# Softmax division moved from each head pair's value sum to the output product of 128 queries

## The chip, the cores and the metric

The kernel runs on one core of one Trainium2 chip. The metric is the device time of one execution in microseconds; lower is better.

## The reference

Three parts work on `x` of shape (4, 1024, 256), each adding to the running result: a linear recurrence, an attention part, and a gated sparse feed-forward part that is used twice, ahead of the attention and behind it (called f1 and f2 in the kernel). The change lies in the attention:

```python
q = (x @ Wq.T).reshape(b, t, N_HEADS, HEAD_DIM)          # 8 heads of 64
kv_latent = x @ Wkv_down.T                                # 64 wide
k = (kv_latent @ Wk_up.T).reshape(b, t, N_HEADS, HEAD_DIM)
v = (kv_latent @ Wv_up.T).reshape(b, t, N_HEADS, HEAD_DIM)
scores = jnp.einsum('bqhd,bkhd->bhqk', q, k) * scale
attn = jax.nn.softmax(scores, axis=-1)
out = jnp.einsum('bhqk,bkhd->bqhd', attn, v)
return out.reshape(b, t, N_HEADS * HEAD_DIM) @ Wo.T
```

A softmax row is exp(s - max) divided by the sum of those exponentials. The sum over keys with the values is linear, so the division may be done at any point between the exponentials and the product with `Wo`. It has to be done per query and head.

## The kernel before, in words

The key and value up-projections are folded into the query and output weights, so that keys and values are the 64-wide latent itself. Four things run one after the other: the recurrence; the start of f1 with the first attention weights; a long stage (about 378 to 1331 us) in which the attention of four batches is the main thread and the rest of f1 and the first steps of f2 are side threads; and f2 (1331 us to the end).

In the long stage `heads()` is a generator that yields once per score tile. It loops over halves `nb` of a batch's 1024 queries, head pairs `g`, and query tiles `q` of 128 queries; inside, over the two heads `j` of the pair. One step is: four matmuls (L881) give scores of 128 queries by 1024 keys in a PSUM tile `sc`; DVE takes the negated row maximum `nm` (L885); ACT takes the exponential into `pr` and accumulates the row sum (L889). The exponentials must then be turned so that keys lie on partitions. For odd `q` the PE does it (`ptp`, L900) and ACT or DVE copies the result to `p` (L903, L905). For even `q` ACT rounds to fp16 (L892), POOL computes the remainder (L893), and a transposing DMA issued by SP brings both to `d` (L894).

The value sums are done later, in `values_sum()`, from two lists: `pending` for odd `q` (one step later) and `late` for even `q` (some steps later). A sum is 32 fp32 matmuls or 48 fp16 matmuls, 64 columns of the array for each head (L925), into a PSUM tile `pmo`. `heads()` is made anew for each batch, and what is left in both lists is summed at the end of each batch (L912).

The division of before: DVE takes the reciprocal of the two row sums (L919), POOL spreads each over 64 columns into `rows` (L921), the PE transposes `rows` into the second half of `pmo` (L933), ACT copies that to `rb` (L935), and DVE multiplies the sum by `rb` into `on` (L936), an SBUF tile that holds four head pairs of 128 queries.

`output()` takes `on` when all four pairs are there: ACT casts it to `onp0` (L945), POOL computes the rest `onp1` (L946), 12 matmuls form the product with the output weights (`pmy`, by `products`, L170), DVE adds it to `x` (L948).

PSUM has three rings in this stage: `sc` with two score tiles, `t` with two tiles for `ptp`, and `s` with two tiles for everything else: `pmo`, `pmy`, the query products and all side threads. Tiles of a ring are given out in the order in which the program asks.

`merge()` sets that order: after each step of `heads()` it takes the side generators that are due. A side entry is (first step, generator, distance to its next step). On top of this a scheduler orders each engine's instructions by simulated time, so that instructions of neighbouring steps can pass each other. `output()` of the first half of a batch is due at step 33 of 64, with a distance of 1.5; that of the second half 1.5 steps into the next batch, for the last batch one step before its end. The last batch's last two query tiles come after `merge()`, followed by the last half of `f2.head`.

Of the kernel before, what the change touches and what calls it, by code (L numbers as in the profile page):

```python
# [10 lines left out]
F32 = mybir.dt.float32  # L11
I32 = mybir.dt.int32
F32R = mybir.dt.float32r
BF16 = mybir.dt.bfloat16
F16 = mybir.dt.float16
AF = mybir.ActivationFunctionType
ALU = mybir.AluOpType
# [4 lines left out]
P = 128  # L22
B = 4
# [6 lines left out]
HEADS = 8  # L30
HD = 64
PAIRS = HEADS // 2
# [132 lines left out]
def products(nc, dst, pairs, start=True, stop=True):  # L165


    terms = [(x, y) for a, b in pairs for x, y in ((a[0], b[0]), (a[0], b[1]), (a[1], b[0]))]
    for i, (x, y) in enumerate(terms):
        nc.tensor.matmul(dst, x, y, start=start and i == 0, stop=stop and i == len(terms) - 1)  # L170
# [19 lines left out]
STEPS = 64  # L190
# [582 lines left out]
class Attention:  # L773
    def __init__(self, tc, x, ident, ident64, wqk, wvo, wd, sp, wp):
        self.nc, self.x, self.ident, self.ident64 = tc.nc, x, ident, ident64
        self.wqk, self.wvo, self.wd, self.sp, self.wp = wqk, wvo, wd, sp, wp
        self.hp = None
        self.k, self.xnt, self.qs, self.on = {}, {}, {}, {}

        self.sident = wp.tile([HD, HD], F32R, tag="sident", name="sident")  # L780

# [71 lines left out]
            nc.vector.tensor_tensor(qs[other, j, :], pm[mine, :], qs[mine, j, :].bitcast(F32), ALU.subtract)  # L853
        yield

    def heads(self, b, psum):

        nc, sp, wp = self.nc, self.sp, self.hp  # L860
        kh, kl, la, lb = self.k[b]
        late, pending = [], []
        for nb, g, q in ((nb, g, q) for nb in range(2) for g in range(PAIRS) for q in range(4)):
            by_dma = q % 2 == 0
            if g == 0:
                self.on[b, nb, q] = wp.tile([P, PAIRS, P], F32, tag=f"on{q}", name=f"on{q}")
            qs = self.qs[b, nb, g]
            ssum = sp.tile([P, 2], F32, tag="ssum", name="ssum", bufs=4)
            if by_dma:
                pts = [wp.tile([P, 2 * TPB, P], F16, tag=f"d{j}", name=f"d{j}", bufs=2) for j in range(2)]  # L870
                parts = ((0, lb[0]), (TPB, lb[0]), (0, lb[1]))
                terms = [(v[:, c, :], i + c) for c in range(TPB) for i, v in parts]
            else:
                pts = [wp.tile([P, TPB, P], F32, tag=f"p{j}", name=f"p{j}") for j in range(2)]
                terms = [(la[:, c, :], c) for c in range(TPB)]
            for j in range(2):
                sc = psum.tile([P, T], "sc", "sc")
                for i, kk in enumerate((kh, kl)):
                    for kb in range(2):
                        sl = slice(kb * 512, (kb + 1) * 512)  # L880
                        nc.tensor.matmul(  # L881
                            sc[:, sl], qs[:, j, q * P : (q + 1) * P], kk[:, sl], start=(i == 0), stop=(i == 1)
                        )
                nm = sp.tile([P, 1], F32, tag="nm", name="nm", bufs=4)
                nc.vector.tensor_reduce(nm, sc, AX.X, ALU.max, negate=True)  # L885
                if by_dma:
                    nc.vector.tensor_scalar(nm, nm, PSHIFT * math.log(2.0), None, ALU.add)  # L887
                pr = wp.tile([P, T], F32, tag="pr", name="pr", bufs=3)
                nc.scalar.activation(pr, sc, AF.Exp, bias=nm, accum_out=ssum[:, j : j + 1])  # L889
                if by_dma:  # L890
                    pd = wp.tile([P, 2, T], F16, tag="pd", name="pd", bufs=2)
                    nc.scalar.copy(pd[:, 0, :], pr)  # L892
                    nc.gpsimd.tensor_tensor(pd[:, 1, :], pr, pd[:, 0, :], ALU.subtract)  # L893
                    nc.sync.dma_start_transpose(pts[j], pd.rearrange("p i k -> p (i k)"))  # L894
                else:
                    for half in range(2):
                        pt = psum.tile([P, 4, P], "t", "ptp")
                        for kk in range(4):
                            kc = 4 * half + kk
                            nc.tensor.transpose(pt[:, kk, :], pr[:, kc * P : (kc + 1) * P], self.ident)  # L900
                        dst = pts[j][:, 4 * half : 4 * half + 4, :]
                        if half == 0 and b == B - 1:
                            nc.vector.tensor_copy(dst, pt)  # L903
                        else:
                            nc.scalar.copy(dst, pt)  # L905
                if j == 0 and pending:
                    self.values_sum(*pending.pop(0), psum)
                if j == 1 and late and by_dma:
                    self.values_sum(*late.pop(0), psum)
                yield  # L910
            (late if by_dma else pending).append((pts, terms, ssum, self.on[b, nb, q][:, g, :]))
        for args in late + pending:  # L912
            self.values_sum(*args, psum)

    def values_sum(self, pts, terms, ssum, on, psum):

        nc, sp = self.nc, self.sp
        rs = sp.tile([P, 2], F32, tag="rs", name="rs")
        nc.vector.reciprocal(rs, ssum)  # L919
        rows = sp.tile([P, 2, HD], F32, tag="rows", name="rows")  # L920
        nc.gpsimd.tensor_copy(rows, rs[:, :, None].to_broadcast([P, 2, HD]))  # L921
        po = psum.tile([P, 2, P], "s", "pmo")
        for n, (v, c) in enumerate(terms):
            for j in range(2):
                nc.tensor.matmul(  # L925
                    po[j * HD : (j + 1) * HD, 0, :],
                    v,
                    pts[j][:, c, :],
                    start=(n == 0),
                    stop=(n == len(terms) - 1),  # L930
                )

        nc.tensor.transpose(po[:, 1, :], rows.rearrange("p j d -> p (j d)"), self.ident)  # L933
        rb = sp.tile([P, P], F32, tag="rb", name="rb", bufs=1)
        nc.scalar.copy(rb, po[:, 1, :])  # L935
        nc.vector.tensor_tensor(on, po[:, 0, :], rb, ALU.mult)  # L936

    def output(self, b, nb, psum, tiles=range(4)):

        nc = self.nc  # L940
        for q in tiles:
            xt = self.x[b * TPB + nb * 4 + q]
            py = psum.tile([P, D], "s", "pmy")
            on = [self.hp.tile([P, PAIRS, P], F32R, tag=f"onp{i}", name=f"onp{i}") for i in range(2)]
            nc.scalar.copy(on[0], self.on[b, nb, q])  # L945
            nc.gpsimd.tensor_tensor(on[1], self.on[b, nb, q], on[0].bitcast(F32), ALU.subtract)  # L946
            products(nc, py, [([t[:, g, :] for t in on], [t[:, g, :] for t in self.wvo]) for g in range(PAIRS)])
            nc.vector.tensor_tensor(xt, xt, py, ALU.add)  # L948
            yield

# [78 lines left out]
def tile_kernel(ctx: ExitStack, tc: tile.TileContext, x_in, w_lru, vecs_in, rows, w_ffn, lin_t, w_attn, w_down, out):  # L1029
    nc = tc.nc  # L1030
# [31 lines left out]
    f2 = Ffn("f2", tc, bp, x, w)  # L1062

    with ExitStack() as c1:
        psum = Banks(c1.enter_context(tc.tile_pool(name="ps1", space=PSUM)), {"pu": 2, "po": 2, "py": 2, "pt": 2})
# [15 lines left out]
        for k in range(NBLK):  # L1081
# [11 lines left out]
            b = k // CH + 1  # L1093
# [24 lines left out]
    with ExitStack() as c2:  # L1118
# [51 lines left out]
        fp = c2.enter_context(tc.tile_pool(name="f_s", bufs=2))  # L1170
        side = []
        for b in range(B):
            n = STEPS * b
            side += [
                (n + nb * 32 + 8 * g - 7, at.queries(b, nb, g, psum, "s"), 1)
                for nb in range(2)
                for g in range(PAIRS)
                if b or nb or g
            ]
            side.append((n + 33, at.output(b, 0, psum), 1.5))  # L1180
            side.append((n + STEPS - 1 if b == B - 1 else n + STEPS + 1.5, at.output(b, 1, psum, range(2 if b == B - 1 else 4)), 1 if b == B - 1 else 1.5))
            side.append((n + 40 if b == B - 1 else n + STEPS + 24, f2.head(2 * b, sp, psum, "s"), 2))
            last = b == B - 1
            side.append((n + STEPS if last else n + STEPS + 8, f2.head(2 * b + 1, sp, psum, "s", (0,) if last else (0, 1)), 1 if last else 2))
            if b < B - 1:
                side.append((n + 38, chain(at.prepare(b + 1, 0, psum, "s"), at.values(b + 1, 0, psum, "s")), 1.5))
                side.append((n + 56, chain(at.prepare(b + 1, 1, psum, "s"), at.values(b + 1, 1, psum, "s")), 1.5))
        side.append((1, at.values(0, 1, psum, "s"), 1))
        for i in range(TPB, NT):
            n = i - TPB  # L1190
            start = 1 + 6.75 * n if n < TPB else STEPS * (n // TPB) - STEPS + 48.25 + 8 * (n % TPB + 1)
            side.append((start, f1.tile(i, fp, psum, "sss", parts=wfs, fine=True), [1, 1, 1, 1, 1, 2, 1]))
        merge(chain(*(at.heads(b, psum) for b in range(B))), side)
        run(at.output(B - 1, 1, psum, range(2, 4)), f2.head(NBLK - 1, sp, psum, "s", (1,)))
    with ExitStack() as c3:
        psum = Banks(c3.enter_context(tc.tile_pool(name="ps3", space=PSUM)), {"pl": 2, "px": 3, "pf": 3})
# [105 lines left out]
```

## Time and profile before

| | |
|---|---|
| median of 3 runs | 1536.99 us (1534.27 to 1539.68) |
| the profiled execution | 1533.81 us, span 1532.1 us |
| mean granted PE clock | 0.941 |
| busy, share of the span | PE 85%, DVE 77%, ACT 66%, POOL 44% |
| instructions | PE 10136, DVE 3674, ACT 2145, POOL 848 |

The shares are averages over all four parts of the kernel. A row of a group names the line, the engine, the operation, the tile written and the tiles read, then the number of instructions, their busy time together and the mean time of one, and last the idle time of the engine just before them with what ended it. A wait is given as "engine, tile, line waited for engine, tile, line: us in total, times, longest". PE means matmuls and transposes, DVE VectorE, ACT ScalarE, POOL GpSimd, SP the queue that issues the DMAs here.

### The profile page before, as it was taken

The page shows a single profiled execution, that of the slowest core. Times are in us where ns is not written, and L with a number is a line of the kernel's source. Part 1 is how long each engine was busy: PE and PEld are TensorE (multiplying, and loading weights), DVE is VectorE, ACT ScalarE, POOL GpSimd, SP SyncE. Part 2 cuts the span into 40 slices and gives each one's busy share as a digit, 9 for nine tenths or more (in the row PEclk, how much of TensorE's full clock was granted, in tenths as well). Part 3 has the DMA queues.
Part 4 walks back from the last instruction along what each step waited for, and adds up shares of the span by engine and source line. Part 5 has one row for each costly group of instructions (what it writes and reads, how often), then busy time and mean ns, then how long its engine had stood idle before and what let it go on. Part 6 is the DMA issues. An engine that isn't in the chain of part 4 may idle for free. (4 is left out here: it accounts for less than half of the span.)

```text
span 1532.1 us, 28693 instructions
## 1 busy us (share of the span) xinstructions
PE 1297.4 (85%) x10136; PEld 960.2 (63%) x10136; DVE 1182.9 (77%) x3674; ACT 1014.5 (66%) x2145; POOL 681.6 (44%) x848
## 2 busy tenths in 40 slices
PE   4879998698898898898998889888999998657786
PEld 3635455365676766766776767677777776334554
DVE  8976665697878887878778687777676675499998
ACT  5353433664787777787777787877777776476664
POOL 2033333162545454544543554454443534157776
PEclk9999999698999999999999999999999999789888
DMA  3010000331454334344433345434444454000000
GB/s 117 32 41 15 21 21 14 135 101 44 76 91 90 70 70 80 67 80 77 85 76 60 65 85 81 66 60 85 78 75 88 83 95 83 1 11 24 25 25 28
DMA packets 288609, 96.51 MB, mean 63 GB/s; under 512 B 268233, under 2 KB 284626, under 8 KB 288466
## 3 DMA queue, kind: packets, MB, share of 16 engines
q1 hardware_dynamic: 283024, 88.50, 29.0%
q10 hardware_dynamic: 5442, 6.18, 1.2%
q8 instruction: 80, 1.31, 0.3%
q14 instruction: 63, 0.52, 0.1%
HBM read 16.01 MB, written 11.53 MB: 18 GB/s over the span
## 5 line engine op out<-in xcount | busy, mean ns | idle before, releaser
L893 POOL TENSOR_TENSOR pd<-pr,pd 128x1024 f16<-128x1024 f32 x128 | 273.5, 2142 | 256.5 <-ACT pd L892 198.6
L885 DVE TENSOR_REDUCE nm<-sc 128x1 f32<-128x1024 f32 x256 | 308.5, 1218 | 76.8 <-PE sc L881 75.3
L889 ACT ACTIVATE pr<-sc,nm 128x1024 f32<-128x1024 f32 x256 | 285.9, 1120 | 89.8 <-DVE nm L887 53.3
L881 PE MATMUL sc<-kh,qs 128*128 128x512 f32 x512 | 184.9, 439 | 27.1 <-ACT pr L889 19.5
L881 PE MATMUL sc<-kl,qs 128*128 128x512 f32 x512 | 162.4, 398 | 0.0
L674 DVE MATCH_REPLACE8 wk<-m,wk 128x256 f32<-128x256 f32 x384 | 158.3, 419 | 0.1
L905 ACT COPY p<-ptp 128x512 f32<-128x512 f32 x224 | 124.3, 590 | 46.3 <-PE ptp L900 38.2
L900 PE MATMUL ptp<-ident,pr 128*128 128x128 f32 x1024 | 140.2, 277 | 15.6 <-ACT pr L889 14.8
L674 DVE MAX8 m<-wk 128x8 f32<-128x256 f32 x384 | 153.0, 424 | 0.4
L925 PE MATMUL pmo<-p,la 128*64 128x128 f32 x2048 | 142.3, 287 | 5.6 <-ACT ft L524 2.9
L900 PEld LDWEIGHTS ptp<-ident,pr 128*128 128x128 f32 x1024 | 117.1, 141 | 38.0 <-ACT pr L889 24.9
L892 ACT CAST pd<-pr 128x1024 f16<-128x1024 f32 x128 | 133.3, 1055 | 5.9 <-DMA d<-pd 4.8
L925 PEld LDWEIGHTS pmo<-p,la 128*64 128x64 f32 x2048 | 121.5, 143 | 24.2 <-ACT ft L524 5.1
L881 PEld LDWEIGHTS sc<-kh,qs 128*128 128x128 f32 x512 | 85.6, 196 | 51.9 <-ACT pr L889 30.8
L881 PEld LDWEIGHTS sc<-kl,qs 128*128 128x128 f32 x512 | 97.1, 190 | 23.4 <-issue 1.4
L925 PE MATMUL pmo<-d,lb 128*64 128x128 f16 x3072 | 101.8, 221 | 7.6 <-DVE qs L853 2.5
L925 PEld LDWEIGHTS <-lb 128*64 128x64 f16 x3072 | 91.2, 111 | 25.4 <-issue 19.5
L628 POOL TENSOR_TENSOR ex<-ex,wk 128x512 f32<-128x512 f32 x61 | 77.6, 1273 | 50.8 <-DVE wk L674 41.7
L921 POOL COPY rows<-rs 128x128 f32<-128x128 f32 x128 | 36.2, 295 | 125.5 <-PE pmo L933 69.3
L936 DVE TENSOR_TENSOR on<-pmo,rb 128x128 f32<-128x128 f32 x128 | 36.5, 285 | 66.8 <-ACT rb L935 66.2
L699 PE MATMUL pf<-wf,vt 128*128 128x256 f32 x288 | 84.4, 438 | 3.6 <-ACT vt L697 3.6
L147 PE MATMUL pt<-ident,xn 128*128 128x128 f32 x256 | 48.2, 308 | 42.5 <-ACT xn L145 30.6
(306 smaller groups left out, 2789.0 us busy)
## 6 DMA issues: line engine op xcount, KB each, us to landing
tt<-ft SPq DMA_DIRECT2D x16, 256.0 KB
tt<-tt SPq DMA_DIRECT2D x8, 512.0 KB
out<-x SPq DMA_DIRECT2D x32, 128.0 KB
x<-in_x ACTq DMA_DIRECT2D x6, 512.0 KB
pf<-pfs SPq DMA_DIRECT2D x12, 256.0 KB
full<-pf SPq DMA_DIRECT2D x24, 128.0 KB
d<-pd SPq DMA_TRANSPOSE x128
wa<-in_w_attn SPq DMA_DIRECT2D x2, 640.0 KB
```

The costliest lines, as they stand in the source:

```text
L147: nc.tensor.transpose(pt[:, k, i * P : (i + 1) * P], xn[:, k * P : (k + 1) * P], ident)
L628: pool.tensor_tensor(ex, ex, wk, ALU.subtract)
L674: ins = make(*args).ins
L699: nc.tensor.matmul(dst, vt[:, k, :], w.wf[:, k, :], start=(k == 0 and bias is None), stop=(k == KD - 1))
L881: nc.tensor.matmul(sc[:, sl], qs[:, j, q * P : (q + 1) * P], kk[:, sl], start=(i == 0), stop=(i == 1))
L885: nc.vector.tensor_reduce(nm, sc, AX.X, ALU.max, negate=True)
L889: nc.scalar.activation(pr, sc, AF.Exp, bias=nm, accum_out=ssum[:, j : j + 1])
L892: nc.scalar.copy(pd[:, 0, :], pr)
L893: nc.gpsimd.tensor_tensor(pd[:, 1, :], pr, pd[:, 0, :], ALU.subtract)
L900: nc.tensor.transpose(pt[:, kk, :], pr[:, kc * P : (kc + 1) * P], self.ident)
L905: nc.scalar.copy(dst, pt)
L925: nc.tensor.matmul(po[j * HD : (j + 1) * HD, 0, :], v, pts[j][:, c, :], start=(n == 0), stop=(n == len(terms) - 1),)
```

## The change

The row sums are kept for all eight heads of a query tile (`ssum0` to `ssum3`, one column per head). `values_sum()` only sums, and ACT copies the undivided sum from PSUM to `on`. The division moves to `output()`: one reciprocal of eight columns on DVE, one broadcast to 128 x 512 on POOL, four PE transposes into a new PSUM tile `pmr` of the ring `s`, and one DVE product of 128 x 512 in place on `on`. A `yield` is put after the product, so that `output()` has two steps for each tile, and its distance goes from 1.5 (1 for the last) to 0.7. `heads()` becomes one generator over all batches; what is left in the two lists at a batch's end is summed in the first steps of the next batch, and the final loop over them runs once. The second half's `output()` is due at 1 step into the next batch, and one `f2.head` entry of the last batch two steps later.

```diff
-    def heads(self, b, psum):
+    def heads(self, psum):
...
-        for nb, g, q in ((nb, g, q) for nb in range(2) for g in range(PAIRS) for q in range(4)):
+        for b, nb, g, q in (
+            (b, nb, g, q) for b in range(B) for nb in range(2) for g in range(PAIRS) for q in range(4)
+        ):
+            kh, kl, la, lb = self.k[b]
...
+                self.sums[b, nb, q] = sp.tile([P, HEADS], F32, tag=f"ssum{q}", name=f"ssum{q}", bufs=2)
...
-                nc.scalar.activation(pr, sc, AF.Exp, bias=nm, accum_out=ssum[:, j : j + 1])
+                h = 2 * g + j
+                nc.scalar.activation(pr, sc, AF.Exp, bias=nm, accum_out=self.sums[b, nb, q][:, h : h + 1])
...
-    def values_sum(self, pts, terms, ssum, on, psum):
-
-        nc, sp = self.nc, self.sp
-        rs = sp.tile([P, 2], F32, tag="rs", name="rs")
-        nc.vector.reciprocal(rs, ssum)
-        rows = sp.tile([P, 2, HD], F32, tag="rows", name="rows")
-        nc.gpsimd.tensor_copy(rows, rs[:, :, None].to_broadcast([P, 2, HD]))
-        po = psum.tile([P, 2, P], "s", "pmo")
+    def values_sum(self, pts, terms, on, psum):
+
+        nc = self.nc
+        po = psum.tile([P, P], "s", "pmo")
...
-        nc.tensor.transpose(po[:, 1, :], rows.rearrange("p j d -> p (j d)"), self.ident)
-        rb = sp.tile([P, P], F32, tag="rb", name="rb", bufs=1)
-        nc.scalar.copy(rb, po[:, 1, :])
-        nc.vector.tensor_tensor(on, po[:, 0, :], rb, ALU.mult)
+        nc.scalar.copy(on, po)
...
     def output(self, b, nb, psum, tiles=range(4)):
...
+            rs = sp.tile([P, HEADS], F32, tag="rs", name="rs")
+            nc.vector.reciprocal(rs, self.sums[b, nb, q])
+            rows = sp.tile([P, HEADS, HD], F32, tag="rows", name="rows", bufs=1)
+            nc.gpsimd.tensor_copy(rows, rs[:, :, None].to_broadcast([P, HEADS, HD]))
+            pb = psum.tile([P, PAIRS, P], "s", "pmr")
+            for g in range(PAIRS):
+                nc.tensor.transpose(
+                    pb[:, g, :], rows[:, 2 * g : 2 * g + 2, :].rearrange("p j d -> p (j d)"), self.ident
+                )
+            on = self.on[b, nb, q]
+            nc.vector.tensor_tensor(on, on, pb, ALU.mult)
+            yield
...
-            side.append((n + 33, at.output(b, 0, psum), 1.5))
-            side.append((n + STEPS - 1 if b == B - 1 else n + STEPS + 1.5, at.output(b, 1, psum, range(2 if b == B - 1 else 4)), 1 if b == B - 1 else 1.5))
...
+            side.append((n + 33, at.output(b, 0, psum), 0.7))
+            side.append((n + STEPS - 1 if last else n + STEPS + 1, at.output(b, 1, psum, range(2 if last else 4)), 0.7))
...
-            side.append((n + STEPS if last else n + STEPS + 8, f2.head(2 * b + 1, sp, psum, "s", (0,) if last else (0, 1)), 1 if last else 2))
+            side.append((n + STEPS + 2 if last else n + STEPS + 8, f2.head(2 * b + 1, sp, psum, "s", (0,) if last else (0, 1)), 1 if last else 2))
...
-        merge(chain(*(at.heads(b, psum) for b in range(B))), side)
+        merge(at.heads(psum), side)
```

More of the change, by code (lines that the diff above doesn't have):

```diff
@@ L777, in __init__ @@
         self.hp = None
-        self.k, self.xnt, self.qs, self.on = {}, {}, {}, {}
+        self.k, self.xnt, self.qs, self.on, self.sums = {}, {}, {}, {}, {}
         self.sident = wp.tile([HD, HD], F32R, tag="sident", name="sident")
@@ L854, in queries @@
         yield
-    def heads(self, b, psum):
+    def heads(self, psum):
         nc, sp, wp = self.nc, self.sp, self.hp
-        kh, kl, la, lb = self.k[b]
         late, pending = [], []
-        for nb, g, q in ((nb, g, q) for nb in range(2) for g in range(PAIRS) for q in range(4)):
+        for b, nb, g, q in (
+            (b, nb, g, q) for b in range(B) for nb in range(2) for g in range(PAIRS) for q in range(4)
+        ):
+            kh, kl, la, lb = self.k[b]
             by_dma = q % 2 == 0
@@ L866, in heads @@
                 self.on[b, nb, q] = wp.tile([P, PAIRS, P], F32, tag=f"on{q}", name=f"on{q}")
+                self.sums[b, nb, q] = sp.tile([P, HEADS], F32, tag=f"ssum{q}", name=f"ssum{q}", bufs=2)
             qs = self.qs[b, nb, g]
-            ssum = sp.tile([P, 2], F32, tag="ssum", name="ssum", bufs=4)
             if by_dma:
@@ L910, in heads @@
                 yield
-            (late if by_dma else pending).append((pts, terms, ssum, self.on[b, nb, q][:, g, :]))
+            (late if by_dma else pending).append((pts, terms, self.on[b, nb, q][:, g, :]))
         for args in late + pending:
             self.values_sum(*args, psum)
-    def values_sum(self, pts, terms, ssum, on, psum):
-        nc, sp = self.nc, self.sp
-        rs = sp.tile([P, 2], F32, tag="rs", name="rs")
-        nc.vector.reciprocal(rs, ssum)
-        rows = sp.tile([P, 2, HD], F32, tag="rows", name="rows")
-        nc.gpsimd.tensor_copy(rows, rs[:, :, None].to_broadcast([P, 2, HD]))
-        po = psum.tile([P, 2, P], "s", "pmo")
+    def values_sum(self, pts, terms, on, psum):
+        nc = self.nc
+        po = psum.tile([P, P], "s", "pmo")
         for n, (v, c) in enumerate(terms):
@@ L925, in values_sum @@
                 nc.tensor.matmul(
[L926 to L930, printed above, removed]
-                )
-        nc.tensor.transpose(po[:, 1, :], rows.rearrange("p j d -> p (j d)"), self.ident)
-        rb = sp.tile([P, P], F32, tag="rb", name="rb", bufs=1)
-        nc.scalar.copy(rb, po[:, 1, :])
-        nc.vector.tensor_tensor(on, po[:, 0, :], rb, ALU.mult)
+                    po[j * HD : (j + 1) * HD, :], v, pts[j][:, c, :], start=(n == 0), stop=(n == len(terms) - 1)
+                )
+        nc.scalar.copy(on, po)
     def output(self, b, nb, psum, tiles=range(4)):
-        nc = self.nc
+        nc, sp = self.nc, self.sp
         for q in tiles:
             xt = self.x[b * TPB + nb * 4 + q]
+            rs = sp.tile([P, HEADS], F32, tag="rs", name="rs")
[10 more added lines that the diff above has]
+            yield
             py = psum.tile([P, D], "s", "pmy")
[L944 to L947, printed above, removed]
+            parts = [self.hp.tile([P, PAIRS, P], F32R, tag=f"onp{i}", name=f"onp{i}") for i in range(2)]
+            nc.scalar.copy(parts[0], on)
+            nc.gpsimd.tensor_tensor(parts[1], on, parts[0].bitcast(F32), ALU.subtract)
+            products(nc, py, [([t[:, g, :] for t in parts], [t[:, g, :] for t in self.wvo]) for g in range(PAIRS)])
             nc.vector.tensor_tensor(xt, xt, py, ALU.add)
@@ L1172, in tile_kernel @@
         for b in range(B):
-            n = STEPS * b
+            n, last = STEPS * b, b == B - 1
             side += [
@@ L1179, in tile_kernel @@
             ]
-            side.append((n + 33, at.output(b, 0, psum), 1.5))
-            side.append((n + STEPS - 1 if b == B - 1 else n + STEPS + 1.5, at.output(b, 1, psum, range(2 if b == B - 1 else 4)), 1 if b == B - 1 else 1.5))
-            side.append((n + 40 if b == B - 1 else n + STEPS + 24, f2.head(2 * b, sp, psum, "s"), 2))
-            last = b == B - 1
-            side.append((n + STEPS if last else n + STEPS + 8, f2.head(2 * b + 1, sp, psum, "s", (0,) if last else (0, 1)), 1 if last else 2))
+            side.append((n + 33, at.output(b, 0, psum), 0.7))
+            side.append((n + STEPS - 1 if last else n + STEPS + 1, at.output(b, 1, psum, range(2 if last else 4)), 0.7))
+            side.append((n + 40 if last else n + STEPS + 24, f2.head(2 * b, sp, psum, "s"), 2))
+            side.append((n + STEPS + 2 if last else n + STEPS + 8, f2.head(2 * b + 1, sp, psum, "s", (0,) if last else (0, 1)), 1 if last else 2))
             if b < B - 1:
```

## The prediction

> **What bounds the kernel now.** I read the stretches first: the span cut at the borders of the attention batches, with the busy time of each engine. In its columns "x" is the number of instructions, PEclk the granted clock.
>
> ```profile
> core 0: us, PE busy (x) PEld busy (x) DVE busy (x) ACT busy (x) POOL busy (x), PEclk, DMA share, GB/s
> 400.00:609.00 209.00, 187.92 (x1901) 148.31 (x1901) 168.93 (x441) 166.77 (x336) 106.36 (x109) 0.99 0.47 82
> 609.00:838.00 229.00, 204.77 (x2010) 163.12 (x2009) 177.14 (x472) 173.80 (x350) 106.86 (x109) 0.97 0.39 74
> ...
> 1066.00:1295.00 229.00, 210.99 (x2295) 170.86 (x2289) 153.12 (x313) 171.62 (x310) 96.26 (x83) 1.00 0.45 80
> 1295.00:1331.00 36.00, 21.22 (x164) 15.67 (x164) 15.75 (x59) 14.10 (x27) 7.43 (x8) 0.73 0.16 30
> ```
>
> All that changes lies between 395 us (first values sum) and 1331 us (the second feed-forward part's batch norm waits for the last output tile). Until 1295 us the PE is busy 87 to 92%, DVE and ACT 67 to 81%. So an edit there is worth what it takes from PE's own row, or from PE's idle time. After 1295 us nothing is full: that stretch is a chain of single instructions, and there latency counts. From 1331 us DVE is busy 191 of 201 us with top-k; the change touches none of it.
>
> Next, who ended PE's waits from 400 to 1310 us, and which DVE and ACT waits belong to the edited lines:
>
> ```profile
> PE sc L881 <- ACT pr L889: 16.7, 21, 1.5
> PE ptp L900 <- ACT pr L889: 14.8, 17, 1.8
> PE pt L147 <- DVE qs L853: 9.1, 5, 2.1
> ...
> PE pmy L170 <- DVE on L936: 1.5, 1, 1.5
> PE pt L147 <- DVE on L936: 1.3, 1, 1.3
> ...
> ACT rb L935 <- PE pmo L933: 23.6, 21, 4.0
> ...
> DVE on L936 <- ACT rb L935: 66.2, 41, 4.3
> DVE rs L919 <- ACT pr L889: 20.4, 22, 2.2
> ```
>
> The reader is to see that DVE stands 66.2 us before L936, yet PE waits for L936 itself only 1.5 + 1.3 + 0.6 + 0.5 = 3.9 us: the big wait is DVE's spare time. All of PE's waits that a DVE instruction ended sum to 41.8 us in that view; those on ACT to some 49 us, exponentials first.
>
> Then the groups of those lines, 400 to 1300 us:
>
> ```profile
> L933 PE MATMUL pmo<-ident,rows 128*128 128x128 f32 x125 | 41.5, 332 | 0.0
> L936 DVE TENSOR_TENSOR on<-pmo,rb 128x128 f32<-128x128 f32 x126 | 35.9, 285 | 66.8 <-ACT rb L935 66.2
> L919 DVE RECIPROCAL rs<-ssum 128x2 f32<-128x2 f32 x126 | 15.2, 153 | 20.9 <-ACT pr L889 20.4 <-issue 0.3
> L935 ACT COPY rb<-pmo 128x128 f32<-128x128 f32 x126 | 34.1, 270 | 22.8 <-PE pmo L933 19.5 <-DVE on L936 2.7
> L921 POOL COPY rows<-rs 128x128 f32<-128x128 f32 x126 | 35.7, 295 | 123.8 <-PE pmo L933 69.3 <-DVE rs L919 29.2 <-DVE nm L887 13.4
> ```
>
> [...]inside a values sum (128*64) matmuls start every 26 to 36 ns, but the first full-width instruction after one starts 150 ns (fp16) or 203 ns (fp32) later, whether it is L933 or another. [...] The trace shows 285 ns for 128 columns, 684 ns for 512 (`kl<-pml,kh`, L161)[...].
>
> **The change, part by part.**
>
> *PE.* The 128 transposes at L933 go, and 128 come back, four in a row per query tile, 32 times. Removed: from the start of L933 to the start of the next instruction, waits taken out, the timeline gives a median of 86 ns after an fp32 sum and 165 ns after an fp16 sum, and 23.5 us over all 128. [...] Added: transposes in a row start every 109 ns (`ptp`, L900), so 32 x 4 x 0.113 = 14.5 us. PE balance: -9.0 us, straight off the fullest engine.
>
> *DVE.* Gone are 128 x (0.153 + 0.285) = 56.1 us; new are 32 reciprocals of eight columns (0.16) and 32 products of 512 columns (0.684): 27.0 us. That is -29 us of busy time, and the 66.2 us wait goes with L936. On the path: the 3.9 us that PE waited for L936, plus PE's other DVE waits (38 us) shrinking with DVE's load in this stage (about 710 us by the windows), 29/710 = 4%, 1.5 us. Sum -5 us. Bounds: 0, if the queue refills, and -15, if the 12 us in which a finished score tile waited behind L936 or L919 for its maximum (summed from the timeline) all passed on, beside those 3.9.
>
> *ACT.* 128 copies stay (266 ns, same shape), now writing `on` itself. Each may start when the sum ends, without L933 (328 ns) between, and not after L936 frees `rb` (2.7 us of waits). ACT's 23.6 us wait shrinks by at most 21 x 0.33 = 7 us; ACT ends about half of PE's waits, and a seventh of that reaches it: -1 us, bounds 0 and -7. The sums accumulate into another column: no cost.
>
> *POOL, queues, buffers.* 128 x 0.295 = 37.8 us of broadcasts become 32 of 512 columns[...]. POOL is under half busy and PE never waits for L921: zero, bounds 0 and -1. SP issues the same transfers; only 1.8 us of PE wait is for them. The sum's "s" buffer is freed without L936 (saving what those 3.9 us already count); the new `pmr` takes one of the two "s" buffers 32 times, for four transposes, a DVE queue and 0.68 us, about 2 us each.
>
> *Batch borders.* Today heads() ends with each batch and its last two sums are emitted before the next batch's first scores. At 613.24 to 616.94 us they run back to back on PE while no score runs; the idle time around them is 1.32 us. With one generator they follow the next scores: about -0.7 us three times, -2 us; bounds 0 and -6.
>
> *Stage*: -9 - 5 - 1 - 2 = **-17 us**.
>
> *The tail, 1295 to 1331 us.* With steps of 0.7 the second output tile is emitted after the main loop's last two sums, where steps of 1 emitted it before, so it moves behind them in the two-buffer "s" rotation. In the trace of before the second tile's `x` is ready at 1305.6 us, its norm at 1309.8, and L529 at 1312.1. In the new order of instructions PE does both sums first, then the second tile's four transposes. From the end of the last sum, at about 1304.9 us (today 1307.5; PE is spared 1.4 us of output products, and waits less): transposes 0.6, product 0.7, ACT cast 0.65, POOL difference 1.3, output products 1.4 to 2, add 0.5, norm chain 4.2, L145 to L529 2.3. That puts L529 near 1316.8 us, +4.7. Behind L529 PE has the third tile's transposes, DVE's product waits for the batch-norm statistics before it, then again cast and difference: in the trace of before the third tile's products start 1.04 us after L529 because its operands were ready; now they end about 3 us later. Sum **+7 us**; bounds +2 (the last sums come earlier than I think) and +10.
>
> Total: -17 + 7 = -10 us. The profiled execution took 1533.81 us (span 1532.1), so it would become 1524. It lies 3.2 us below the median of the runs, inside their spread of 5.4 us; against the median 1536.99 the forecast is **1527 us**.
>
> **The rivals.**
>
> *Twice the gain.* If every DVE microsecond ahead of a score maximum counts (-15 instead of -5), the ACT wait passes whole (-7 instead of -1) and the borders give -6, the stage gives -37 and the sum is -30: 1507 us. For it: PE is paced by a loop of scores, maximum, exponential. Against: the maxima wait for PE (`DVE nm L885 <- PE sc L881`, 69.6 us), so DVE is early more often than late.
>
> *No net effect.* PE's gain of 9 us alone comes true and the tail takes 7 to 10: 1535 to 1538 us. For it: PE's waits are mostly on exponentials, which nothing relieves.
>
> *Slower: a standing ACT.* The cast `onp<-on` on ACT used to find its input ready (ACT waited 0.7 us for L936). Now it waits for the product, which stands in DVE's order behind a 1.22 us maximum and needs `rows` from POOL, where a 2.14 us difference may be ahead. Behind the cast on ACT stand exponentials and `ptp` copies, for which PE waits. At 1.2 us for each of 28 casts and all of it passed on: +34, total +24, 1561 us; half passed on, +7, 1544 us. It decides from the point where a cast costs PE 0.53 us (28 x 0.53 = 15 us, which turns -10 into +5). Against: reciprocals and broadcasts are ordered several score steps ahead, and ACT has a quarter of its time free.
>
> *That the change doesn't do what it says* is out: the built order holds 32 products and 32 broadcasts where there were 128 each, and four transposes in a row.
>
> **How the numbers follow.** Moderate gain (1519 to 1531 us): 0.50. Twice the gain: 0.14. No net effect: 0.16. Standing ACT: 0.20. A measurement of this kernel can tell about 0.3% (4.6 us) from no change. Faster 0.50 + 0.14 = 0.64, same 0.16, slower 0.20. The range 1509 to 1546 us leaves out about half of the twice-gain case and under half of the slower case.
>
> **What would show it.** Right, step by step: PE busy from 400 to 1295 us down by some 9 us; no DVE wait of tens of us at the on-writing line; the `on` product near 0.68 us x 32[...]; the first top-k batch norm 7 us later after the last score matmul than the 37 us of today. Wrong: PE waits for exponentials above 31.5 us, or long ACT waits at the `onp` cast (the standing ACT); a tail as short as today's; or PE waits ended by DVE cut by half (twice the gain).

## The result, and the profile after

The changed kernel takes **1574.62 us** (median of 4 runs, 1572.69 to 1576.84) against 1538.34 us of the kernel before on the same chip: ratio 1.024, 95% interval 1.0213 to 1.0268. It is slower, where the forecast said 1527 us. The profiled execution took 1572.97 us (span 1571.2).

To place the loss I cut both spans at instructions that both kernels have: the **stage** from the first row maximum (`nm`) to the last, the **tail** from there to the first L587 of the last `f2.head` (the first activation behind the second part's batch norm), and what lies ahead of the stage and behind the tail.

| us | before | after | difference |
|---|---|---|---|
| stage | 914.9 | 944.1 | +29.2 |
| of it PE idle (gaps over 0.06 us) | 94.7 | 116.2 | +21.5 |
| of it PE at work | 820.2 | 828.0 | +7.8 |
| tail | 35.6 | 45.1 | +9.5 |
| ahead of the stage | 380.4 | 378.7 | -1.7 |
| behind the tail | 201.2 | 203.3 | +2.1 |

Cut further by score steps, +20.5 of the +29.2 lie in the first 16 of each 32 steps, where the four output products of a half batch run, and +8.7 in the other 16. First the stretches of the kernel after, with the columns as before (busy time and instructions of PE, PE's weight loads, DVE, ACT, POOL, then clock, DMA share, GB/s):

```profile
400.00:609.00 209.00, 190.07 (x1862) 149.18 (x1858) 163.99 (x388) 164.48 (x335) 101.19 (x86) 0.98 0.41 82
609.00:838.00 229.00, 196.26 (x1894) 157.60 (x1896) 161.94 (x392) 165.12 (x330) 99.11 (x81) 0.95 0.35 70
...
1066.00:1295.00 229.00, 203.02 (x2216) 165.49 (x2214) 151.44 (x277) 164.50 (x304) 87.03 (x55) 0.99 0.38 75
1295.00:1331.00 36.00, 28.50 (x322) 23.44 (x324) 17.47 (x26) 22.22 (x40) 15.12 (x9) 1.00 0.43 89
```

PE, DVE and ACT are all less busy between 609 and 838 us than before, and PE handles 1894 matmuls there instead of 2010: no engine has become the bound, the same work has spread out. The last row shows the stage still running where the tail used to lie. Then the waits of the kernel after, 400 to 1340 us:

```profile
DVE nm L887 <- PE sc L883: 131.6, 89, 4.6
...
PE ptp L903 <- ACT pr L892: 20.8, 18, 5.5
...
PE sc L883 <- ACT pr L892: 17.7, 26, 2.6
POOL rows L938 <- PE pmr L941: 17.2, 7, 6.7
...
ACT onp L949 <- DVE nm L889: 10.0, 4, 5.0
...
PE pmr L941 <- DVE qs L853: 8.5, 4, 3.3
...
PE pmy L170 <- ACT onp L949: 6.2, 7, 2.3
```

Three things to see. The big DVE wait at the line that writes `on` is gone, but DVE now stands 131.6 us before the row maxima, where it stood 69.6: its spare time moved. PE's waits for exponentials (the `ptp` and `sc` lines) are 38.5 us where they were 31.5. And the last three lines are new or nearly so: the cast `onp` waits for DVE, PE's output product for that cast (0.6 us before), and PE's `pmr` for DVE's `qs`, which reads another tile of the ring `s`. The groups of the new lines, 400 to 1300 us:

```profile
L927 ACT COPY on<-pmo 128x128 f32<-128x128 f32 x121 | 32.6, 273 | 24.4 <-PE pmo L924 23.0 <-POOL onp L950 1.2
L945 DVE TENSOR_TENSOR on<-on,pmr 128x512 f32<-128x512 f32 x28 | 19.0, 678 | 4.6 <-PE pmr L941 4.4 <-ACT pr L892 0.2
L949 ACT CAST onp<-on 128x512 fp32r<-128x512 f32 x28 | 17.4, 622 | 14.3 <-DVE nm L889 10.0 <-DVE on L945 1.7 <-PE pmy L170 1.7
L938 POOL COPY rows<-rs 128x512 f32<-128x512 f32 x28 | 17.4, 621 | 26.7 <-DVE rs L936 16.0 <-PE pmr L941 10.5
L941 PE MATMUL pmr<-ident,rows 128*128 128x128 f32 x112 | 17.3, 275 | 8.9 <-DVE qs L853 8.5 <-ACT ex L615 0.4
```

The wide product costs what the prediction said (678 ns); the wide broadcasts took 621 ns each, 17.4 us in this window, where the narrow ones of before took 35.7. So the loss is not in the durations of these instructions. This points to the order. The timeline of the kernel after, at one of the output products:

```profile
760.42 1.86 PE L170 MATMUL pmy<-wvo,onp 128*128 128x256 f32 x12
...
762.12 0.60 PE L941 MATMUL pmr<-ident,rows 128*128 128x128 f32 x4
...
764.54 0.68 DVE L945 TENSOR_TENSOR on<-on,pmr 128x512 f32<-128x512 f32 x1
...
765.30 0.62 ACT L949 CAST onp<-on 128x512 fp32r<-128x512 f32 x1 [5.02 <-DVE nm L889]
...
765.98 0.51 PE L170 MATMUL pmy<-wvo,onp 128*128 128x256 f32 x2 [2.33 <-ACT onp L949]
...
766.32 0.60 PE L941 MATMUL pmr<-ident,rows 128*128 128x128 f32 x4
```

PE turns the divisors of the next tile (`pmr`) only once it has come to the product of this one (`pmy`), and this one's product needs the cast, the cast DVE's product, and that this tile's own `pmr`. The four tiles of a half batch form one chain. ACT stands 5.02 us before the cast (an exponential queued behind it also needed DVE here), PE 2.33 us before `pmy`.

### The profile page after: what moved, and what is told of

Same layout as the page of the kernel before. It is cut to its first block, busy times and chain, and to the rows that moved or that the text cites. A ratio compares the mean times of both kernels' runs of the same rounds, so it can differ in the third digit from the quotient of the medians.

```text
span 1571.2 us, 28314 instructions
## 1 busy us (share of the span) xinstructions
PE 1303.9 (83%) x10136; PEld 971.0 (62%) x10136; DVE 1174.1 (75%) x3482; ACT 1010.8 (64%) x2145; POOL 665.2 (42%) x752
## 4 chain that ended last, share of the span: by engine, by line
DVE 39%; PE 38%; ACT 11%; issue 4%; DMA 3%; POOL 3%; ACTq 0%; SPq 0%; POOLq 0%; DVEq 0%
DVE wk L674 10%; PE pmo L924 8%; PE sc L883 8%; DVE m L674 8%; DVE nm L887 7%; PE ptp L903 4%; ACT pr L892 3%; PE po L437 2%; PE pmy L170 2%; DVE qs L853 2%; PE pu L170 2%; DMA d<-pd 2%; ACT pd L895 1%; PE pz L452 1%; POOL pd L896 1%
## 5 line engine op out<-in xcount | busy, mean ns | idle before, releaser
L903 PE MATMUL ptp<-ident,pr 128*128 128x128 f32 x1024 | 150.9, 284 | 28.1 <-ACT pr L892 20.8
L883 PE MATMUL sc<-kl,qs 128*128 128x512 f32 x512 | 168.8, 411 | 0.0
L903 PEld LDWEIGHTS ptp<-ident,pr 128*128 128x128 f32 x1024 | 120.3, 145 | 55.3 <-ACT pr L892 29.5
L908 ACT COPY p<-ptp 128x512 f32<-128x512 f32 x224 | 129.0, 594 | 36.3 <-PE ptp L903 25.4
L674 DVE MAX8 m<-wk 128x8 f32<-128x256 f32 x384 | 149.5, 416 | 0.4
L699 PEld LDWEIGHTS pf<-wf,vt 128*128 128x128 f32 x288 | 58.9, 213 | 29.1 <-ACT vt L697 14.9
L556 PE MATMUL pl<-lint,xc_f 128*128 128x512 f32 x128 | 71.8, 648 | 5.3 <-ACT xc_f L587 5.3
```

What stands on the lines that cost most here:

```text
L556: self.last_logits = nc.tensor.matmul(v, x, w.lint, start=False, stop=True).ins
L674: ins = make(*args).ins
L699: nc.tensor.matmul(dst, vt[:, k, :], w.wf[:, k, :], start=(k == 0 and bias is None), stop=(k == KD - 1))
L883: nc.tensor.matmul(sc[:, sl], qs[:, j, q * P : (q + 1) * P], kk[:, sl], start=(i == 0), stop=(i == 1))
```

## The theories and the experiments

**Theory (chained tiles).** The first eight runs led to this theory; the expectations of those runs still weigh others, by letters that they explain. Of the later runs `changed_pmr_in_t` was set up to test it. `pmr` shares the two buffers `s` with `pmy`, and tiles of a ring are given out in program order: `pmr` of tile q+1 comes after `pmy` of tile q. With the division ahead of the cast, the tiles' chains run one after another, and the other users of `s` (sums, queries, side work) wait with them. **Rivals:** a standing ACT, whatever the buffers (the cast waits for DVE); the single generator; the 0.7 steps; the mere load of 32 more tiles in `s`.

### The parts of the change alone

`one_gen` is the kernel before with the single generator only; `div_only` moves the division only, with heads() per batch, the old due times and distances and no new yield; `div_gen` adds the single generator to that, `div_pace` instead the yield and the 0.7 steps with their due times (all three are called "the 0.7 steps" from here on). Of `div_only`, against the changed kernel:

```diff
             nc.vector.tensor_tensor(on, on, pb, ALU.mult)
-            yield
...
-            side.append((n + 33, at.output(b, 0, psum), 0.7))
+            side.append((n + 33, at.output(b, 0, psum), 1.5))
...
-        merge(at.heads(psum), side)
+        merge(chain(*(at.heads(b, psum) for b in range(B))), side)
```

Expected of `one_gen`: 

> The kernel before, with heads() as one generator over all four batches and nothing else changed. Theory A (the division's new place costs: the cast on ACT stands behind the DVE product): no division is moved, so within 5 us of 1538. Theory B (the batch border: sums that used to be flushed now push into the next batch): most of the +36 us is here, 1560 to 1575. Theory C (the new distances of output() in the list of side steps): within 5 us of 1538. Theory D (the written order of the instructions as a whole is a matter of luck; any edit shifts it): anything from 1525 to 1560, without a wait that is common to the slow ones.

Expected of `div_only`: 

> The division moved to output(), but heads() made anew for each batch and the old distances (1.5, 1), with no yield between product and cast. Theory A: nearly all of the loss of the stage, 1560 to 1572, and ACT stands before the cast as in the changed kernel (14 us). Theory B and C: within 8 us of 1538. The tail should be as short as before (36 us from the last row maximum to the top-k norm), because both first output tiles are again emitted ahead of the last sums. Theory D: 1525 to 1560.

Expected of `div_gen`: 

> The changed kernel with the old distances (1.5, 1), old due steps and no yield between product and cast: division moved and one generator. Theory C says 1540 or less (the new distances are the cause). Theory A says 1560 to 1570, theory B 1560 to 1575. In each case the tail is some 9 us shorter than in the changed kernel (36 instead of 45 us), if the tail's cost is the place of the second output tile behind the last sums.

Expected of `div_pace`: 

> The changed kernel with heads() made anew for each batch: division moved and the new distances of 0.7. Theory B says 1540 to 1547 (only the tail's 9 us stay). Theories A and C say 1565 to 1577, with the long tail of 45 us.

Measured: `one_gen` 1537.52 us, 1.0011 (1.0000 to 1.0022); `div_only` 1585.77 us, 1.0323 (1.0293 to 1.0353); `div_gen` 1592.0 us, 1.0364 (1.0334 to 1.0394); `div_pace` 1560.84 us, 1.0161 (1.0131 to 1.0190). The generator alone changes next to nothing, so the -2 us of the batch borders was not there. The moved division alone costs 49 us, more than the whole change: the 0.7 steps win 25 us of it back. `div_only` and `div_gen` came out 14 and 22 us above what their expectations allowed theory A. The chain is plainest in the timeline of `div_only`:

```profile
766.50 0.68 DVE L943 TENSOR_TENSOR on<-on,pmr 128x512 f32<-128x512 f32 x1
768.27 0.64 ACT L946 CAST onp<-on 128x512 fp32r<-128x512 f32 x1
768.99 1.28 POOL L947 TENSOR_TENSOR onp<-on,onp 128x512 fp32r<-128x512 f32 x1 [1.93 <-ACT onp L946]
...
770.32 1.45 PE L170 MATMUL pmy<-wvo,onp 128*128 128x256 f32 x10 [0.55 <-POOL onp L947]
...
773.79 0.41 DVE L949 TENSOR_TENSOR x<-x,pmy 128x256 f32<-128x256 f32 x1
...
774.25 0.66 PE L939 MATMUL pmr<-ident,rows 128*128 128x128 f32 x4 [1.02 <-DVE x L949]
774.95 0.69 DVE L943 TENSOR_TENSOR on<-on,pmr 128x512 f32<-128x512 f32 x1 [0.35 <-PE pmr L939]
775.73 0.62 ACT L946 CAST onp<-on 128x512 fp32r<-128x512 f32 x1 [0.70 <-DVE on L943]
```

Read downwards it is one tile's product, cast, remainder, output product and add, and then the next tile's `pmr`, which PE starts 0.05 us after the add that frees the buffer. In `div_only` 14 of 21 such `pmr` begin no earlier than 0.3 us before the end of the add of the tile ahead; in the changed kernel, where the chain is looser, 6 of 21.

### Cutting the links of the chain

`no_division` is `div_only` without reciprocal, broadcast, transposes and product: the attention stays undivided. `scratch_product` has all of them, but the product goes to a tile that nobody reads, so the cast takes the undivided `on`. `pmr_in_ring_t` is `div_only` with one word altered:

```diff
-            nc.vector.tensor_tensor(on, on, pb, ALU.mult)
+            junk = sp.tile([P, PAIRS, P], F32, tag="junk", name="junk", bufs=1)
+            nc.vector.tensor_tensor(junk, on, pb, ALU.mult)
```

```diff
-            pb = psum.tile([P, PAIRS, P], "s", "pmr")
+            pb = psum.tile([P, PAIRS, P], "t", "pmr")
```

Expected of `no_division`: 

> div_only (1585.8) with the whole division left out: no reciprocal, broadcast, transposes or product; the row sums are still accumulated, and the output is not divided. It prices the cheap value sum alone. Theory A (the loss is in the chain inside output(): transposes, product, cast, difference, products) says 1515 to 1535: the prediction's gain of PE and DVE without its costs. Theory E (the sum that ACT copies out is itself slower, for instance because ACT now stands where DVE stood) says 1555 or more.

Expected of `scratch_product`: 

> div_only with the product written to a scratch tile that nobody reads: every instruction stays, with its engine and size, only the cast and the difference of on no longer wait for it (the output is not divided). Theory A1 (the wait of ACT's cast for DVE's product is the cost) says 1530 to 1548. Theory A2 (the new PSUM tile pmr blocks the ring s while it waits for DVE) says 1575 to 1590, since pmr is held just as long. In between, both share.

Expected of `pmr_in_ring_t`: 

> div_only with pmr taken from the ring t (which holds the transposed exponentials) instead of s. Theory A2 says 1540 to 1560; theory A1 says no change, 1578 to 1592; if t is the tighter ring it gets worse.

Measured: `no_division` 1512.25 us, 0.9836 (0.9766 to 0.9905); `scratch_product` 1530.49 us, 0.9969 (0.9955 to 0.9984); `pmr_in_ring_t` 1532.27 us, **0.9964 (0.9948 to 0.9980)**. The division's instructions themselves cost about 18 us (1530.5 against 1512.3; the interval of `no_division` is 10 us to either side), but waiting for their result costs another 55 (1585.8 against 1530.5), and nearly all of that goes when `pmr` alone is put in the other ring. `scratch_product` keeps `pmr` in `s` and holds it as long (1.95 us on average, 2.09 in `div_only`), so neither that hold nor the load of 32 more tiles in `s` is what costs: the dependence and the shared ring together are. ACT's waits before the casts, 400 to 1300 us, first in `div_only`, then in `pmr_in_ring_t`:

```profile
L946 ACT CAST onp<-on 128x512 fp32r<-128x512 f32 x28 | 17.3, 620 | 11.8 <-DVE on L943 10.6 <-DVE nm L887 0.6 <-PE pmy L170 0.5
```

```profile
L946 ACT CAST onp<-on 128x512 fp32r<-128x512 f32 x30 | 18.7, 625 | 6.0 <-PE pmy L170 3.6 <-DVE on L943 1.3 <-issue 0.7
```

The cast depends on the product in both, but ACT's wait for it went from 10.6 to 1.3 us. So this pair alone does not set a standing ACT apart from the ring, except by size: 10.6 us is a fifth of what was won. The timeline of `pmr_in_ring_t`, at the same kind of place:

```profile
742.48 0.60 PE L939 MATMUL pmr<-ident,rows 128*128 128x128 f32 x4
...
742.84 1.67 PE L170 MATMUL pmy<-wvo,onp 128*128 128x256 f32 x12
743.61 0.68 DVE L943 TENSOR_TENSOR on<-on,pmr 128x512 f32<-128x512 f32 x1
745.36 0.63 ACT L946 CAST onp<-on 128x512 fp32r<-128x512 f32 x1
...
748.63 0.66 PE L939 MATMUL pmr<-ident,rows 128*128 128x128 f32 x4
...
749.09 1.69 PE L170 MATMUL pmy<-wvo,onp 128*128 128x256 f32 x12
```

Now `pmr` stands ahead of the previous tile's `pmy`, and the product is divided while that one is multiplied and added. Over the stage `pmr` starts 5.46 us before the previous tile's add ends (mean of 21), in `div_only` 0.2 us. The whole gain lies where the output products run: 52.2 us in the first 16 of each 32 score steps, 0.5 in the others. PE's waits for the cast, 400 to 1340 us, first in `div_only`, then in `pmr_in_ring_t`:

```profile
PE pmy L170 <- ACT onp L946: 14.4, 9, 3.0
```

```profile
PE pmy L170 <- ACT onp L946: 1.6, 5, 0.6
```

This version beats both kernels, though by 4 us only.

### The division as side work of its own

`divide_apart` keeps `pmr` in `s`, but divides all four tiles of a half batch first (steps 33 to 36) and casts and multiplies them from step 36 on, so that no cast waits for a product. In it the last batch's `f2.head` entry reads its two tiles before the second one's output product has been added. `divide_apart_t` puts `pmr` in `t` and that entry one step later.

```diff
-            side.append((n + 33, at.output(b, 0, psum), 1.5))
+            side.append((n + 33, at.divide(b, 0, psum), 1))
+            side.append((n + 36, at.output(b, 0, psum), [2, 1.5, 0.5, 1]))
```

Expected of `divide_apart`: 

> div_only with the division of the four query tiles as side steps of its own (steps 33 to 36 of a half), and cast, difference and output products two to four steps later (36, 38, 40, 40); one of the four on tiles gets a second buffer. The work is the same and the division is done for real. Theory A1 says 1530 to 1548, since the product is long done when the cast's turn comes. Theory A2 says 1570 or more. Theory E as well.

Expected of `divide_apart_t`: 

> The kernel of divide_apart (division of four tiles as side work of its own at steps 33 to 36, casts and output products from step 36 on) with `pmr` in the buffers "t", and the last batch's feed-forward head one step later, so that it follows its tile's output product. If what was left there (stage 936 us, 21 above before) is the load of 32 more users on the two "s" buffers, the stage falls to 912-920 us and the total to 1530-1540 us. If it is the casts and products packed late at steps 36 to 40, nothing much falls: 1550-1558 us. In both cases no cast waits for a product.

Measured: `divide_apart` 1555.45 us, 1.0117 (1.0049 to 1.0184); `divide_apart_t` 1549.01 us, 1.0077 (1.0049 to 1.0105). Breaking the chain by order wins 30 us of `div_only`'s 49 and leaves a loss. Taking `pmr` out of `s` as well (and moving that entry) changes it by 6 us, which is within the intervals; at 1549 us it lies just under the 1550 to 1558 us expected if the load of `s` is not what was left. Casts and products packed late at steps 36 to 40 would fit, but spreading them out was not tried; this stays open.

### The changed kernel, with single words altered

`changed_pmr_in_t` is the changed kernel with `pmr` in `t`. `changed_early_tile` instead cuts the last batch's output steps, so that its second tile is emitted ahead of the last two sums again; `changed_t_early_tile` does both. `t_per_batch_paced` and `t_single_old_steps` are `div_pace` and `div_gen` with `pmr` in `t`.

```diff
-            side.append((n + STEPS - 1 if last else n + STEPS + 1, at.output(b, 1, psum, range(2 if last else 4)), 0.7))
+            side.append((n + STEPS - 1 if last else n + STEPS + 1, at.output(b, 1, psum, range(2 if last else 4)), 0.3 if last else 0.7))
```

Expected of `changed_pmr_in_t`: 

> The changed kernel with one word altered: `pmr` is taken from the PSUM buffers "t" instead of "s"; order, single generator, 0.7 steps and the longer tail stay. Chained-tiles theory (the loss of the stage comes from `pmr` of the next tile standing behind `pmy` of this one in the two "s" buffers): the stage comes back from 944 to 912-920 us, the tail stays near 45 us (9.5 longer than before), so 1540 to 1549 us, 1.001 to 1.008 times before. Rival (a standing ACT because of the wait on the product as such, whatever the buffers): the casts wait as long as now, 1565 to 1575 us. Rival (the single generator and the 0.7 steps are what costs): nothing changes either, 1565 to 1575 us.

Expected of `changed_t_early_tile`: 

> The changed kernel with `pmr` in the buffers "t", and the steps of the last batch's output product cut from 0.7 to 0.3, so that its second tile is emitted ahead of the main loop's last two sums as in the kernel before. If both of the parts named so far (chained tiles in the stage, late second tile in the tail) are the whole loss, the tail falls to 36-39 us and the total to 1531-1540 us, 0.995 to 1.003 times before. If the tail is long for another reason (the third tile's chain behind L529), it stays above 43 us and the total at 1540-1549 us.

Expected of `changed_early_tile`: 

> The changed kernel with only the last batch's output steps cut from 0.7 to 0.3; `pmr` stays in "s". If the two parts add up, this takes 6 to 9 us from the tail alone (45 to 36-39 us) and leaves the stage at 944 us: 1564 to 1570 us, 1.018 to 1.023 times before. If the tail's length comes from `pmr` in the buffers "s" and not from the order of the second tile, no change: 1572-1577 us.

Expected of `t_per_batch_paced`: 

> `pmr` in the buffers "t", heads() called per batch as before, but the changed kernel's 0.7 steps and extra yield in output(). Against pmr_in_ring_t (1532, 0.9964: per batch, old 1.5 steps without the yield) and changed_pmr_in_t (1545, 1.0051: single generator and 0.7 steps). If the 0.7 steps cost the 8 to 12 us between those two, this is 1.003 to 1.007 (1541 to 1547 us); if the single generator costs them, it is 0.996 to 1.000 (1530 to 1536 us).

Expected of `t_single_old_steps`: 

> `pmr` in the buffers "t", the single generator of the changed kernel, but the old steps of 1.5 and 1 and no yield in output(). If the 0.7 steps cost the 8 to 12 us between pmr_in_ring_t and changed_pmr_in_t, this is 0.996 to 1.000 (1530 to 1536 us); if the single generator costs them, 1.003 to 1.007 (1541 to 1547 us); if each gives some, both lie near 1.001.

Measured: `changed_pmr_in_t` 1544.59 us, 1.0051 (1.0035 to 1.0066); `changed_t_early_tile` 1542.85 us, 1.0044 (1.0031 to 1.0057); `changed_early_tile` 1568.96 us, 1.0200 (1.0156 to 1.0244); `t_per_batch_paced` 1543.33 us, 1.0042 (1.0028 to 1.0055); `t_single_old_steps` 1539.78 us, 1.0015 (1.0002 to 1.0028).

| ratio to before | `pmr` in `s` | `pmr` in `t` |
|---|---|---|
| heads() per batch, old steps | 1.0323 | 0.9964 |
| single generator, old steps | 1.0364 | 1.0015 |
| heads() per batch, 0.7 steps | 1.0161 | 1.0042 |
| both (the change) | 1.0240 | 1.0051 |

One word in the changed kernel wins 1.9% (1.024 against 1.0051), 29 us. The chained-tiles theory had said 1540 to 1549 us, both rivals 1565 to 1575. In the profiled executions the stage is 21.5 us shorter (944.1 to 922.6), the tail 5.5 (45.1 to 39.6) and what follows 2.1, while the part ahead of the stage, which the word doesn't touch, came out 2.6 longer. So of the loss of 36 us about 29 goes with the ring. ACT stands before 28 of the casts nearly as long as in the changed kernel (12.9 us against 14.3), though less of it is for DVE (6.5 us against 11.7) and more for the output product ahead. The view of all 32, from 378 to 1330 us:

```profile
L949 ACT CAST onp<-on 128x512 fp32r<-128x512 f32 x32 | 20.0, 624 | 19.5 <-PE pmy L170 11.5 <-DVE on L945 7.7 <-POOL rows L938 0.3
```

One thing stays open here. The stage's 21.5 us come half from the first 16 of each 32 steps (10.5) and half from the others (11.0), where no output product of a half batch is due. How the chain reaches those steps in the changed kernel is not shown.

What is left is the generator and the steps, which the right column shows without the chain: with neither the kernel is 4 us faster than before, with both 8 us slower. Each costs something alone, both together hardly more than the steps. With heads() per batch the 0.7 steps win 25 us where the chain is (left column) and cost 11 where it isn't. Of these 11 the tail is 3.5 us (36.1 in `pmr_in_ring_t`, 39.6 in `t_per_batch_paced`).

My expectation that the tail would stay near 45 us in `changed_pmr_in_t` was wrong: it fell to 39.6. With the second tile early it falls from 45.1 to 38.0 us in `s`, and from 39.6 to 38.0 in `t`. So each of the two remedies takes most of the longer tail by itself, and their shares don't add up. The ratios of the whole can't be told apart from those without the early tile, and `changed_t_early_tile` missed its 1531 to 1540 us: the ring and the late tile are not the whole loss.

## Why the prediction was wrong

**The step that failed** is "POOL, queues, buffers". It named the very thing, that `pmr` takes one of the two `s` buffers 32 times for about 2 us each, and put no price on it. The holds are as long as said (1.98 us on average) and are not the price, as `scratch_product` shows. The ring makes tile q+1's `pmr` follow tile q's `pmy` in PE's order, and `pmy` now depends on `pmr`: a dependence that had been spread over 128 small sums was put behind an output product that must run four times in a row. That price was about 29 us, where 0 was in the sum. What was short in the ring was less the room than a free order: `pmr` in another ring won 29 us, while `scratch_product`, with holds as long in `s`, stays at 0.9969 of before.

**The slower rival** was on the right side but with the wrong mechanism. It priced ACT's wait at the cast, deciding from 0.53 us each. ACT's wait there measured 14.3 us for 28 casts, 0.51 us each, just under that point, while the stage lost 29 us. PE's waits for exponentials passed 31.5 us, the sign that the prediction had named for this rival; yet with `pmr` in `t` ACT still stands 12.9 us before those casts, 6.5 of them for DVE's product, and the loss is gone for the most part.

**PE, -9 us: not seen.** L933 (23.5 us) is gone as said. But in `pmr_in_ring_t`, where nothing chains, PE at work in the stage is 820.6 us, against 820.2 before. The same 1024 score matmuls show why. Groups of the kernel before, then of `pmr_in_ring_t`, 378 to 1330 us (busy, mean ns, idle before):

```profile
L881 PE MATMUL sc<-kh,qs 128*128 128x512 f32 x512 | 184.9, 439 | 27.1 <-ACT pr L889 19.5 <-DVE qs L853 6.7 <-DVE kl L161 0.7
L881 PE MATMUL sc<-kl,qs 128*128 128x512 f32 x512 | 162.4, 398 | 0.0
```

```profile
L881 PE MATMUL sc<-kh,qs 128*128 128x512 f32 x512 | 187.5, 446 | 20.9 <-ACT pr L890 13.4 <-DVE qs L853 6.4 <-DVE kl L161 0.7
L881 PE MATMUL sc<-kl,qs 128*128 128x512 f32 x512 | 168.1, 410 | 0.0
```

The same instructions took 187.5 + 168.1 - 184.9 - 162.4 = 8.3 us longer. The clock records agree: in the stage PE ran at half clock for 34 us before and for 63 us in `pmr_in_ring_t`. Score matmuls outside these spells took 434 (`kh`) and 394 ns (`kl`) before and 433 and 399 ns after; those that touch one took 610 to 677 ns, and there were 52 where there had been 19. Over all runs the gap is smaller: the mean granted clock of the whole span is 0.938 (34 runs of before) against 0.9345 (17), and among the runs of before 0.01 of clock goes with some 7 us. By this estimate the clock took back some 2.5 us of the 9 on average, and in these two profiles all of it may be the clock; I cannot fix it closer. The 23.5 us of the prediction also hold 5.3 us of 16 transposes that stood right before a wait for something else, where taking them out frees no time by itself. No step of the prediction had PE's clock in it.

**DVE, ACT and borders, -8 us: a wait exchanged for the next.** In `pmr_in_ring_t` PE's waits that DVE ended fell from 42.0 to 25.9 us over the stage, a drop of 16 that even passes the bound of -15. But PE's waits on ACT rose from 50.3 to 64.0. Net, PE's idle time went from 94.7 to 90.8: -3.9. The exponentials ahead of `sc` and `ptp` did come less late (32.4 to 29.2 us). But 8.2 of the added 13.7 us are two waits that the kernel before doesn't have, ahead of the transposes `pt` that prepare the next batch's attention:

```profile
PE pt L147 <- ACT pr L890: 8.2, 2, 4.1
```

In the kernel before `pt` waited 9.1 us for DVE's `qs` instead, a wait that is gone here, so half of DVE's drop was exchanged at one place. The changed kernel has the same two waits. Why they came is not shown.

**The tail, +7 us (bounds +2 and +10): +9.5**, inside its bounds and in the direction given. With the second tile early 7.1 us of it go, which is the order that the prediction worked out; with `pmr` in `t` 5.5 go. So the order is shown to matter, but the 7.1 us, so near to the forecast, hold only together with the ring: with `pmr` in `t` the same early tile wins 1.6.

**What held:** product 0.678 us (0.684 said), L936's wait gone, PE never held up by the broadcast (0.621 us; no row of before has its shape). The exponentials with their sums in another column took 1.120 us, as before. The 150 and 203 ns up to the first full-width instruction after a values sum, which the balance of PE doesn't count as won, are there in the kernel after as well (medians of 67 and 65 sums; only L529 starts after 103 ns). The reciprocal of eight columns took 195 ns where 160 was said (an estimate; 153 ns for two columns and the 1.04 ns a column between the products of 128 and 512 give 159), about 1 us over all. (The 26 to 36 ns between matmuls inside a values sum are medians: in most sums of the kernel before the starts alternate, fp32 between 6 or 7 and 102 or 103 ns, fp16 between 3 or 4 and 52 or 53. No sum rests on it.) POOL does wait 17.2 us for the single buffer of `rows` (in the waits of after), which the prediction had not seen; it is harmless, as `pmr_in_ring_t` has the same wait (18.8 us).

**Bottom line:** stage -17 predicted. Even with the ring put right and the old steps kept it is -3.4 (914.9 to 911.5). Dropping the division altogether takes 20.4 us from the stage (914.9 to 894.5 in `no_division`), so -17 assumed that most of its whole cost would go.

## What to carry to other kernels

When a new PSUM tile joins a ring, don't ask how long it is held; ask which tiles stand before and behind it in that ring, and whether one behind depends on it through other engines. If tile q+1's first step shares a two-buffer ring with tile q's last step, the tiles can run in series, as here: give the new step another ring (29 us won in the changed kernel), or emit it ahead (here all four tiles ahead still left a loss of 19 us). And try a pacing change on its own, since the pacing that helps while a chain is there (25 us here) may cost once the chain is gone (11 us here).

## What the runs showed of the hardware

In the clock records of this stage PE's granted clock is either 1.0 or 0.5. In the kernel before it is 0.5 for 33.6 us: seven spells of 3.41 us, one of 6.83, and the end of one of 10.24 that began ahead of the stage. The longest of PE's gaps that began in the 6 us ahead of a spell was 1.18 to 2.76 us for the eight that began in the stage; in the kernel after, with sixteen such spells, it was 0.73 to 5.52 us. What starts a spell is not shown, and no run set out to test it. The transposes `ptp` start every 109 ns at 1.0 and every 213 ns at 0.5 (medians of the kernel before). Mean clock from 380 to 1300 us, in the stretches of the kernel before, of `div_only` and of `pmr_in_ring_t`:

```profile
380.00:1300.00 920.00, 823.12 (x8276) 655.38 (x8276) 690.89 (x1717) 702.87 (x1370) 427.32 (x419) 0.98 0.43 77
```

```profile
380.00:1300.00 920.00, 799.15 (x7730) 637.09 (x7728) 645.03 (x1487) 671.59 (x1312) 391.09 (x310) 0.95 0.35 73
```

```profile
380.00:1300.00 920.00, 827.24 (x8300) 664.30 (x8300) 681.13 (x1528) 703.14 (x1372) 411.25 (x323) 0.97 0.38 78
```

The run with the chain had less clock as well. `div_only` and `pmr_in_ring_t` have the same instructions, but in their profiles 0.95 and 0.97 of the clock (over all their runs 0.92 and 0.93 of the whole span), and PE at work for 838.1 and 820.6 us of the stage. Of PE's busy time in the stage 76.1 us ran at half clock in the one and 56.0 in the other, against 32.6 before; with the `ptp` starts twice as far apart at half clock, half of that difference of 20 us, about 10 us by this estimate, is work that the slower clock stretched.
